# Attention blocks 2 to 7: layernorm statistics by ScalarE in two accumulating passes, x transposed by 32x32 squares and DMA moves, denominators inverted in a narrow layout

## The chip, the cores and the metric

The kernel runs on one core of a Trainium2 chip. The engines of a core work side by side: TensorE (PE) multiplies matrices into PSUM, VectorE (DVE) and ScalarE (ACT) work on elements, GpSimd (POOL) does a few small operations and issues some of the DMA transfers, SyncE (SP) issues most of them. The metric is the device time of one execution in microseconds (us); less is better.

## The reference

x holds 8 batches of 512 tokens with 512 features in float32. Four parts follow one another, each added to x behind a learned gate:

```python
x = x + tanh(g_xattn[0]) * xattn0(layernorm(x), ctx)      # linear attention, 16 heads of 32
x = x + tanh(g_ffn[0])   * ffn0(layernorm(x))             # 512 -> 2048 -> 512, exact gelu
x = x + tanh(g_xattn[1]) * xattn1(layernorm(x), ctx, mask)# softmax over 64 memory tokens
x = x + tanh(g_ffn[1])   * ffn1(layernorm(x))             # 8 expert groups, top 8 of 32, silu
```

The change touches the first of them alone. There, with f(y) = y + 1 where y > 0 and exp(y) elsewhere:

```python
q    = f(x_norm @ Wq.T)                      # per head
gate = sigmoid(x_norm @ Wg.T + bg)
k, v = f(ctx @ Wk.T), ctx @ Wv.T
z    = 1 / (q . sum_of_k + 1e-6)             # one number per token and head
out  = (q @ (k.T @ v)) * z * gate @ Wo.T
```

## The kernel before, in words

The work is cut into three times eight blocks, one per batch: `xa0` (the linear attention), then `ff0`, then `ff1` (which begins with the softmax attention). A block's x stands in SBUF as 128 partitions x 4 token tiles x 512 features. The large products are computed on PE by a scheme of seven half-size products in place of eight (numbered 1 to 7 in the code; their sums and differences are formed by DVE and ACT). Each `xa0` block has three of them: `QUp` (tiles x_q, w_q, z_q), `GUp` (x_g, w_g, z_g) and `ODown` (x_xa_down, w_xa_down, z_xa_down). Products 1, 6 and 7 of Q and G are copied out of PSUM by ACT (line 928, tiles u1, u6, u7); every product of O is added into x by DVE (line 1048).

The main loop (lines 1409 to 1468) runs over b. Turn b issues Q of block b, G of block b, and O of block b - 1, since O needs the denominators z of its block. Between the products it calls generators: `prep` (`prep_xa0` of block b + 1, which is `normed` and then `token_combinations`), `den` (`denominators`), `gated`, `numerators`, `attended`, and a `builder` that forms weight sums for the ff0 stage on DVE, with loads and stores on SP.

`normed` (lines 475 to 586) makes the normalised and transposed x of a block, xnT. In `xa0` blocks it takes mean and variance of each token by DVE (bn_stats and bn_aggr, four tiles), lets POOL raise the variance to the power -1/2, and normalises on ACT (line 60 in the profile, bias and scale per token). Each normalised tile is transposed by four PE transposes into PSUM (line 524, pt_xa), and ACT copies the result to xnT (line 526). The second way in the same function, used by most blocks of the later stages, has ACT write the tile in a layout of 32x32 squares, DVE transpose the squares in place (line 562), and 16 DMAs of 64 KB move the rows to their partitions. `token_combinations` (lines 680 to 696) forms four sums S of the quarters of xnT on DVE.

`denominators` (lines 1247 to 1266) multiplies q by the sums of the keys on PE (pd, 128 x 512, each of 16 heads repeated in eight rows), adds the small constant and inverts on DVE (lines 1255 and 1258), and stores the 128 x 512 result to DRAM by SP. `spread` reads it back with each head's row copied to the 32 partitions of its features.

The order of instructions on an engine is set before the run. A scheduler with its own cost model orders PE, DVE and ACT in this phase; instructions issued inside `with here("vector")` or the like, and all of POOL's and SP's, keep the order of the program among themselves. Every instruction of an engine waits for those before it. Line 60 is the helper through which such ordered instructions are recorded, so that many groups of the profile carry that line.

Of the kernel before, what the change touches and what calls it, by code (L numbers as in the profile page):

```python
# [30 lines left out]
P = 128  # L31
# [37 lines left out]
def flamingo_kernel(  # L69
# [46 lines left out]
    bank = {"ps": ps, "xn": awork}  # L116
# [110 lines left out]
    for h in range(P // HD):  # L227
        nc.vector.memset(heads[ts(h, HD), ts(h, 8)], 1.0)
    neg_half = const.tile([P, NT], F32, tag="neg_half", name="neg_half")
# [245 lines left out]
    def normed(ph, b, tag, normed_part=lambda t: None):  # L475

        xb = xs[ph, b]
        by_products = ph == "xa0" or tag == "ff0_0"
        xnT = work.tile([P, NC, S] if ph == "xa0" else [P, NC, NT, P], F32, tag="xnT", name=f"xnT_{tag}")
# [3 lines left out]
        ahead = held or ph == "xa0" and b > 0  # L483
        with here(*(["vector"] if held or ph == "xa0" else [])):
            for t in range(NT):
                st = small.tile([P, 6], F32, tag="st", name=f"st_{tag}_{t}")
                nc.vector.bn_stats(st, xb[:, t, :])  # L487
                nc.vector.bn_aggr(mv[:, t, :], st)
        var = small.tile([P, NT], F32, tag="var", name=f"var_{tag}")
        nc.vector.tensor_scalar(var, mv[:, :, 1], LN_EPS, None, ALU.add)  # L490
        rstd = small.tile([P, NT], F32, tag="rstd", name=f"rstd_{tag}")
        if by_scalar:
            shift = small.tile([P, NT], F32, tag="nshift", name=f"nshift_{tag}")
            nc.vector.tensor_scalar(shift, mv[:, :, 0], -1.0, None, ALU.mult)  # L494
# [20 lines left out]
        if by_products:  # L515

            def normed_tile(t):
                xn[t] = bank["xn"].tile([P, D], F32, tag="xn", name=f"xn_{tag}_{t}", bufs=2)
                norm(t, xn[t])

            def turn(t):
# [3 lines left out]
                if ph == "xa0":  # L525
                    nc.scalar.copy(xnT[:, :, ts(t, P)], pt)
# [31 lines left out]
        xn = bank["xn"].tile([P, NC, NT, P], F32, tag="xn", name=f"xn_{tag}")  # L558
# [1101 lines left out]
```

## Time and profile before

| | |
|---|---|
| time, three runs | 2025.08, 2026.78, 2028.16 us; median 2026.78 |
| the profiled execution | 2028.04 us, of which the span of instructions is 2026.3 |
| granted PE clock, mean | 0.999 |
| busy, whole span | PE 99%, PE's weight loads 88%, DVE 75%, ACT 32%, POOL 11% |
| the attention stretch | about 50 to 372 us of the span |

A row of the groups by line reads: line, engine, operation, what is written from what, partitions x elements, how many; then busy us and mean ns of one; then the engine's idle time just ahead of them and what ended it. In a row of the waits, the engine and tile on the left stood idle for what is on the right: us in total, number of times, the longest. A row of the timeline has start, duration, engine, line and instruction; ends of matmuls are modelled, so that the distance from one start to the next says more than the durations.

### The profile page before, as it was taken

How to read it: one execution, taken by the hardware profiler on the slowest of the kernel's cores; microseconds unless marked ns; L12 is line 12 of the kernel's file. 1: busy time of each engine (PE TensorE's matmuls, PEld its weight loads, DVE VectorE, ACT ScalarE, POOL GpSimd, SP SyncE). 2: the span in 40 equal slices, each digit the busy share in tenths (PEclk: the TensorE clock that was granted, in tenths of full speed). 3: DMA queues.
4: the chain of work that ended last, by engine and by line, in shares of the span. 5: the costliest groups of instructions: out<-in, count | busy, mean ns of one | idle time of the engine just before them, and what ended most of it. 6: DMA issues, size and time to landing. Idle time of an engine off the chain costs nothing. (4 is left out here: it accounts for less than half of the span.)

```text
span 2026.3 us, 35088 instructions
## 1 busy us (share of the span) xinstructions
PE 2004.3 (99%) x12428; PEld 1779.3 (88%) x12428; DVE 1509.6 (75%) x3012; ACT 648.2 (32%) x1294; POOL 216.8 (11%) x387
## 2 busy tenths in 40 slices
PE   9999999999999999999999999999999999999998
PEld 5888887899989899999888889898989888898988
DVE  4688888676857677777767687787788786877758
ACT  3543443323242424233234231313232232313121
POOL 3000000101010101011011111110202020110000
PEclk9999999999999999999999999999999999999999
DMA  6466655799999999999987969696978879696865
GB/s 202 138 206 189 186 161 166 235 319 292 317 291 300 301 302 279 299 301 287 296 266 247 307 206 304 204 307 194 305 236 250 277 227 304 191 318 181 280 202 171
DMA packets 318062, 508.81 MB, mean 251 GB/s; under 512 B 42945, under 2 KB 109665, under 8 KB 313793
## 3 DMA queue, kind: packets, MB, share of 16 engines
q1 hardware_dynamic: 302768, 464.05, 72.9%
q0 software_dynamic: 9264, 19.31, 3.5%
q10 hardware_dynamic: 5856, 23.20, 3.2%
q8 instruction: 101, 1.65, 0.3%
q14 instruction: 73, 0.59, 0.1%
HBM read 413.04 MB, written 69.27 MB: 238 GB/s over the span
## 5 line engine op out<-in xcount | busy, mean ns | idle before, releaser
L916 PE MATMUL x_ff<-S_ff,w_ff 128*128 128x256 f32 x1280 | 303.0, 380 | 2.4 <-ACT u_ff L928 2.4
L916 PE MATMUL w_ff<-S_ff,w_ff 128*128 128x256 f32 x1280 | 303.9, 380 | 0.5 <-DVE a_ff L971 0.3
L916 PE MATMUL x_ff<-xnT_ff,w_ff 128*128 128x256 f32 x1280 | 298.5, 381 | 0.0
L928 ACT COPY u_ff<-x_ff 128x512 f32<-128x512 f32 x240 | 140.0, 584 | 447.8 <-PE x_ff L916 412.7
L916 PEld LDWEIGHTS x_ff<-S_ff,w_ff 128*128 128x128 f32 x1280 | 242.7, 190 | 35.5 <-ACT u_ff L928 2.8
L916 PEld LDWEIGHTS w_ff<-S_ff,w_ff 128*128 128x128 f32 x1280 | 241.0, 190 | 36.7 <-issue 2.7
L916 PEld LDWEIGHTS x_ff<-xnT_ff,w_ff 128*128 128x128 f32 x1280 | 240.4, 191 | 33.9 <-issue 2.1
L1111 PE MATMUL x_ff_down<-w_ff_down,split_ff_down 128*128 128x128 f32 x1344 | 162.5, 275 | 1.1 <-DVE split_ff_down L1096 0.9
L1111 PEld LDWEIGHTS x_ff_down<-w_ff_down,split_ff_down 128*128 128x128 f32 x1344 | 156.0, 192 | 1.6 <-DVE split_ff_down L1096 1.1
L916 PE MATMUL z_ff<-xnT_ff,w_ff 128*128 128x256 f32 x640 | 153.1, 380 | 0.0
L1125 DVE TENSOR_TENSOR part_ff_down<-part_ff_down 128x128 f32<-128x128 f32 x315 | 85.1, 289 | 71.3 <-ACT part_ff_down L1138 62.0
L916 PEld LDWEIGHTS z_ff<-xnT_ff,w_ff 128*128 128x128 f32 x640 | 119.8, 190 | 20.6 <-issue 5.3
L495 POOL TENSOR_TENSOR rstd_ff<-var_ff,neg_half 128x4 f32<-128x4 f32 x15 | 15.9, 1061 | 861.7 <-DVE nshift_ff L494 861.7
L1111 PE MATMUL w_ff_down<-w_ff_down,split_ff_down 128*128 128x128 f32 x896 | 107.9, 275 | 0.0
L1111 PEld LDWEIGHTS w_ff_down<-w_ff_down,split_ff_down 128*128 128x128 f32 x896 | 103.9, 192 | 0.0
L976 ACT ACTIVATE a_ff<-a_ff,b_sb 128x256 f32<-128x256 f32 x128 | 58.1, 501 | 92.5 <-DVE a_ff L971 92.5
L1009 DVE TENSOR_TENSOR up_ff<-w_ff,u_ff 128x512 f32<-128x512 f32 x96 | 65.8, 685 | 27.1 <-ACT u_ff L928 27.1
L971 DVE TENSOR_TENSOR a_ff<-w_ff,u_ff 128x512 f32<-128x512 f32 x64 | 44.0, 687 | 54.9 <-ACT u_ff L928 54.4
L1111 PE MATMUL x_ff_down<-w_ff_down,a_ff 128*128 128x128 f32 x672 | 83.5, 275 | 1.0 <-ACT a_ff L60 1.0
L1111 PE MATMUL w_ff_down<-w_ff_down,s_ff 128*128 128x128 f32 x672 | 82.8, 275 | 0.0
L1111 PEld LDWEIGHTS x_ff_down<-w_ff_down,a_ff 128*128 128x128 f32 x672 | 79.7, 192 | 1.8 <-ACT a_ff L60 1.1
L999 DVE SCALAR_TENSOR_TENSOR g_ff<-th_ff,x_ff 128x512 f32<-128x512 f32 x48 | 32.7, 681 | 64.8 <-ACT th_ff L998 64.8
(264 smaller groups left out, 3462.0 us busy)
## 6 DMA issues: line engine op xcount, KB each, us to landing
w_ff_down<-stream_ff SPq DMA_DIRECT2D x680, 256.0 KB
w_ff<-ff_up SPq DMA_DIRECT2D x560, 256.0 KB
stream_ff<-build_ff_down SPq DMA_DIRECT2D x49, 448.0 KB
x_ff<-x_ff SPq DMA_DIRECT2D x16, 1024.0 KB
share<-shares SPq DMA_DIRECT2D x64, 256.0 KB
ff_up<-build_ff_up SPq DMA_DIRECT2D x42, 256.0 KB
x_ff<-x_xa ACTq DMA_DIRECT2D x8, 1024.0 KB
x_ff<-x_ff ACTq DMA_DIRECT2D x8, 1024.0 KB
```

The costliest lines, as they stand in the source:

```text
L495: nc.gpsimd.tensor_tensor(rstd, var, neg_half, ALU.pow)
L916: nc.tensor.matmul(p[:, n, :], lhsT=w[:, c, ts(n, P)], rhs=moving, **self.mark(m, 2 * n + c),)
L928: nc.scalar.copy(self.s[m], p)
L971: nc.vector.tensor_tensor(h, p, s, ALU.add)
L976: nc.scalar.activation(h[:, n, :], p[:, n, :], AF.Gelu, bias=b1_sb[:, f : f + 1])
L999: nc.vector.scalar_tensor_tensor(g, th, 1.0, p, ALU.add, ALU.mult)
L1009: nc.vector.tensor_tensor(u, p, s, ALU.add)
L1111: nc.tensor.matmul(p[bank][:, place, :], lhsT=operand[k][:, c, :], rhs=w[at // 4][:, ts(at % 4, P)], start=bank not in opened, stop=True, ...
L1125: return lambda: nc.vector.tensor_tensor(m(k), m(k), m(by), ALU.add)
```

## The change

Four things change, all in `xa0`.

1. In blocks 2 to 7 the statistics come from ACT. A first pass (Identity with an accumulator, four tiles) gives the sums, DVE turns them into the shift, a second pass (Square with the shift as bias, four tiles) gives the sums of squares; DVE makes the variance of them. Power, shift and normalisation follow as before.
2. In the same blocks x is transposed in the second way of `normed`: squares on DVE, and 16 DMAs, here issued by SP. All `xa0` blocks take over the layout of xnT that the later stages have. Blocks 0 and 1 keep bn_stats and the PE transposes.
3. For blocks 0 to 6 the denominators go from PSUM through ACT (constant added), one row per head by a POOL DMA to DRAM, back as 128 x 64 by a second POOL DMA, through one DVE reciprocal of 128 x 64, and out by a third POOL DMA. `spread` reads 16 rows in place of 128. Block 7 keeps the wide reciprocal and stores 16 rows.
4. The main loop calls `prep` after other products: after Q's n = 0, 1, 3, 4 (at b = 0 only 4) in place of 4, after G's 0, 1, 2 in place of 3, and after O's 1 in place of 0, 1, 3, 5, with the remainder at O's 4.

```diff
--- before.py
+++ after.py
...
     def normed(ph, b, tag, normed_part=lambda t: None):
 
         xb = xs[ph, b]
-        by_products = ph == "xa0" or tag == "ff0_0"
-        xnT = work.tile([P, NC, S] if ph == "xa0" else [P, NC, NT, P], F32, tag="xnT", name=f"xnT_{tag}")
+        by_products = tag in ("xa0_0", "xa0_1", "ff0_0")
+        xnT = work.tile([P, NC, NT, P], F32, tag="xnT", name=f"xnT_{tag}")
         mv = small.tile([P, NT, 2], F32, tag="mv", name=f"mv_{tag}")
         held = ph == "ff0" and b > 1
         by_scalar = tag != "xa0_0"
         ahead = held or ph == "xa0" and b > 0
+        var = small.tile([P, NT], F32, tag="var", name=f"var_{tag}")
+        rstd = small.tile([P, NT], F32, tag="rstd", name=f"rstd_{tag}")
+        if ph == "xa0" and not by_products:
+            sums = small.tile([P, 2, NT], F32, tag="sums", name=f"sums_{tag}")
+            shift = small.tile([P, NT], F32, tag="nshift", name=f"nshift_{tag}")
+            with here():
+                for t in range(NT):
+                    nc.scalar.activation(
+                        temp(f"of_{tag}_{t}"), xb[:, t, :], AF.Identity, accum_out=sums[:, 0, t : t + 1]
+                    )
+            yield
+            nc.vector.tensor_scalar(shift, sums[:, 0], -1.0 / D, None, ALU.mult)
+            with here():
+                for t in range(NT):
+                    nc.scalar.activation(
+                        temp(f"off_{tag}_{t}"),
+                        xb[:, t, :],
+                        AF.Square,
+                        bias=shift[:, t : t + 1],
+                        accum_out=sums[:, 1, t : t + 1],
+                    )
+            yield
+            nc.vector.tensor_scalar(var, sums[:, 1], 1.0 / D, LN_EPS, ALU.mult, ALU.add)
         with here(*(["vector"] if held or ph == "xa0" else [])):
-            for t in range(NT):
+            for t in range(NT if by_products or ph != "xa0" else 0):
                 st = small.tile([P, 6], F32, tag="st", name=f"st_{tag}_{t}")
                 nc.vector.bn_stats(st, xb[:, t, :])
                 nc.vector.bn_aggr(mv[:, t, :], st)
-        var = small.tile([P, NT], F32, tag="var", name=f"var_{tag}")
-        nc.vector.tensor_scalar(var, mv[:, :, 1], LN_EPS, None, ALU.add)
-        rstd = small.tile([P, NT], F32, tag="rstd", name=f"rstd_{tag}")
-        if by_scalar:
-            shift = small.tile([P, NT], F32, tag="nshift", name=f"nshift_{tag}")
-            nc.vector.tensor_scalar(shift, mv[:, :, 0], -1.0, None, ALU.mult)
+        if by_products or ph != "xa0":
+            nc.vector.tensor_scalar(var, mv[:, :, 1], LN_EPS, None, ALU.add)
+            if by_scalar:
+                shift = small.tile([P, NT], F32, tag="nshift", name=f"nshift_{tag}")
+                nc.vector.tensor_scalar(shift, mv[:, :, 0], -1.0, None, ALU.mult)
         nc.gpsimd.tensor_tensor(rstd, var, neg_half, ALU.pow)
         if by_scalar:
             nc.gpsimd.tensor_tensor(shift, shift, rstd, ALU.mult)
...
-                xn[t] = bank["xn"].tile([P, D], F32, tag="xn", name=f"xn_{tag}_{t}", bufs=2)
+                if tag == "xa0_0":
+                    xn[t] = start.tile([P, D], F32, tag="xn", name=f"xn_{tag}_{t}", bufs=2)
+                elif tag == "xa0_1":
+                    if t == 0:
+                        xn["all"] = aunits.tile([P, NT, D], F32, tag="a", name=f"xn_{tag}")
+                    xn[t] = xn["all"][:, t, :]
+                else:
+                    xn[t] = temp(f"xn_{tag}_{t}")
                 norm(t, xn[t])
 
             def turn(t):
                 pt = psum(f"pt_{tag}_{t}").rearrange("p (c q) -> p c q", q=P)
                 for c in range(NC):
                     nc.tensor.transpose(pt[:, c, :], xn[t][:, ts(c, P)], ident)
-                if ph == "xa0":
-                    nc.scalar.copy(xnT[:, :, ts(t, P)], pt)
-                else:
-                    nc.scalar.copy(
-                        xnT[:, :, t].rearrange("p q (c i) -> p c q i", c=NC),
-                        pt.rearrange("p c (q i) -> p c q i", q=NC),
-                    )
+                nc.scalar.copy(
+                    xnT[:, :, t].rearrange("p q (c i) -> p c q i", c=NC),
+                    pt.rearrange("p c (q i) -> p c q i", q=NC),
+                )
 
...
-        xn = bank["xn"].tile([P, NC, NT, P], F32, tag="xn", name=f"xn_{tag}")
+        xn = bank["xn"].tile([P, NC, NT, P], F32, tag=bank["tag"], name=f"xn_{tag}")
...
                 with here("gpsimd"):
-                    queue = nc.sync if tag.startswith("ff1") else nc.gpsimd
+                    queue = nc.sync if ph == "xa0" or tag.startswith("ff1") else nc.gpsimd
                     queue.dma_start(out=xnT[ts(l, HD), q], in_=xn[ts(q, HD), l])
...
-    def features_of(ph, xnT):
-
-        if ph == "xa0":
-            return xnT.rearrange("p c (t q i) -> p c t q i", q=NC, i=HD)
+    def features_of(xnT):
+
         return xnT.rearrange("p q t (c i) -> p c t q i", c=NC)
...
-        if ph == "xa0":
-            v = features_of(ph, xnT).rearrange("p c t q i -> p c t (q i)")
-            a11, a12, a21, a22 = (v[:, ts(h, 2), ts(r, 2)] for r in range(2) for h in range(2))
-            to = s.rearrange("p k c (t i) -> p k c t i", t=2)
-        else:
-            a11, a12, a21, a22 = (xnT[:, :, ts(r, 2), ts(h, 2 * HD)] for r in range(2) for h in range(2))
-            to = s.rearrange("p k c (q t i) -> p k (c q) t i", q=2, t=2)
+        a11, a12, a21, a22 = (xnT[:, :, ts(r, 2), ts(h, 2 * HD)] for r in range(2) for h in range(2))
+        to = s.rearrange("p k c (q t i) -> p k (c q) t i", q=2, t=2)
         nc.vector.tensor_tensor(to[:, 0], a21, a22, ALU.add)
         nc.vector.tensor_tensor(to[:, 1], to[:, 0], a11, ALU.subtract)
         nc.vector.tensor_tensor(to[:, 2], a11, a21, ALU.subtract)
         nc.vector.tensor_tensor(to[:, 3], a12, to[:, 1], ALU.subtract)
-        if ph == "xa0":
-            return to.rearrange("p k c t (q i) -> p k c t q i", i=HD)
         return to.rearrange("p k q t (c i) -> p k c t q i", c=2)
...
         z = temp(f"z_{b}")
-        nc.vector.tensor_scalar(z, pd, ATT_EPS, None, ALU.add)
-        yield
-        for r in range(2):
-            nc.vector.reciprocal(z[:, ts(r, H2)], z[:, ts(r, H2)])
+        of_heads = z.rearrange("(n k) t -> n k t", k=8)[:, 0, :]
+        over[b] = dram.tile([P // 8, S], F32, tag=f"over{b}", name=f"over_{b}")
+        if b == B - 1:
+            nc.vector.tensor_scalar(z, pd, ATT_EPS, None, ALU.add)
             yield
-        over[b] = dram.tile([P, S], F32, tag=f"over{b}", name=f"over_{b}")
-        nc.sync.dma_start(out=over[b], in_=z)
+            for r in range(2):
+                nc.vector.reciprocal(z[:, ts(r, H2)], z[:, ts(r, H2)])
+                yield
+            nc.sync.dma_start(out=over[b], in_=of_heads)
+            yield
+            return
+        nc.scalar.activation(z, pd, AF.Identity, bias=eps, scale=1.0)
+        under = dram.tile([P // 8, S], F32, tag=f"under{b}", name=f"under_{b}")
+        narrow = small.tile([P, S // 8], F32, tag="narrow", name=f"narrow_{b}")
+        with here("gpsimd"):
+            nc.gpsimd.dma_start(out=under, in_=of_heads)
+            nc.gpsimd.dma_start(out=narrow, in_=under.rearrange("n (u q) -> (n u) q", u=8))
+        yield
+        yield
+        nc.vector.reciprocal(narrow, narrow)
+        with here("gpsimd"):
+            nc.gpsimd.dma_start(out=over[b].rearrange("n (u q) -> (n u) q", u=8), in_=narrow)
+        yield
         yield
 
     def spread(b):
 
-        rows = over[b].rearrange("(c h k) t -> c k h t", c=NC, k=8)
+        rows = over[b].rearrange("(c h) t -> c h t", c=NC)
         over[b] = aunits.tile([P, NC, S], F32, tag="over", name=f"spread_{b}")
         for h in [slice(0, 2), slice(2, 4)] if b == B - 1 else [slice(0, 4)]:
             for c in range(NC):
-                nc.sync.dma_start(out=over[b][ts(c, HD), h], in_=rows[c, 0, h].partition_broadcast(HD))
+                nc.sync.dma_start(out=over[b][ts(c, HD), h], in_=rows[c, h].partition_broadcast(HD))
...
+    bank.update(xn=aunits, tag="over")
...
             if n == 4:
                 flush()
-                if b < B - 1:
-                    some(prep)
+            if n in ((4,) if b == 0 else (0, 1, 3, 4) if b < B - 1 else ()):
+                some(prep)
             tick()
         if done:
             attended(done[0], done[2], numerators(*done[0:2]))
...
                     load_x("ff0", 1)
             if b == B - 1 and n > 3:
                 next(den, None)
-            if n == 3 or n > 3 and not done:
+            if n in ((0, 1, 2) if b < B - 1 else (3,)) or n > 2 and not done:
                 some(prep)
         if not done:
             for _ in den:
...
             elif n == 6:
                 attended(b, g.th, pn, gated)
                 combine_inner(slice(0, 2), "x")
-            if n in ((0, 1, 3, 5) if b < B - 1 else (6,)):
+            if n in ((1,) if b < B - 1 else (6,)):
                 some(prep)
+            if n == 4 and b < B - 1:
+                for _ in prep:
+                    pass
             tick()
         for _ in prep:
             pass
...
```

More of the change, by code (lines that the diff above doesn't have):

```diff
@@ L115, in flamingo_kernel @@
     kvp = first.enter_context(tc.tile_pool(name="kvp", bufs=2, space=PSUM))
-    bank = {"ps": ps, "xn": awork}
+    bank = {"ps": ps}
     def psum(name):
@@ L228, in flamingo_kernel @@
         nc.vector.memset(heads[ts(h, HD), ts(h, 8)], 1.0)
+    eps = const.tile([P, 1], F32, tag="eps", name="eps")
+    nc.vector.memset(eps, ATT_EPS)
     neg_half = const.tile([P, NT], F32, tag="neg_half", name="neg_half")
@@ L737, in cross_attention @@
                     lhsT=ctxT[:, c, :],
-                    rhs=features_of("ff1", xnT)[:, c].rearrange("p (u r) q i -> p r u q i", r=2)[:, r],
+                    rhs=features_of(xnT)[:, c].rearrange("p (u r) q i -> p r u q i", r=2)[:, r],
                     start=c == 0,
@@ L797, in prep_ff1 @@
                     lhsT=router_sb[:, c, :],
-                    rhs=features_of("ff1", xnT)[:, c, t],
+                    rhs=features_of(xnT)[:, c, t],
                     start=c == 0,
@@ L902, in product @@
             xnT, s = blocks[self.ph, self.b][0:2]
-            v = features_of(self.ph, xnT)
+            v = features_of(xnT)
             (w,) = self.weights(m)
@@ L1535, in flamingo_kernel @@
     hpool = stack(tc.tile_pool(name="inner", bufs=1, reuse_waits="tile"))
-    bank["xn"] = hpool
+    bank.update(xn=hpool, tag="xn")
     router_sb = hpool.tile([P, NC, E], F32, tag="router_w", name="router_sb")
```

## The prediction

> **What bounds the kernel now.** I read the page's head, then the waits of TensorE (PE) from 0 to 400 us, the stretch that holds the attention blocks, then the groups by line there, then timelines.
>
> ```profile
> span 2026.3 us, 35088 instructions
> ...
> PE 2004.3 (99%) x12428; PEld 1779.3 (88%) x12428; DVE 1509.6 (75%) x3012; ACT 648.2 (32%) x1294; POOL 216.8 (11%) x387
> ```
>
> PE works 99% of the span; 22 us in all are idle. Time is won only by taking instructions off PE or ending one of its few waits, and any new wait of PE lengthens the span one for one. Its waits in this stretch, and the groups that the change touches:
>
> ```profile
> PE x_g L916 <- ACT u_g L928: 1.8, 3, 1.2
> ...
> PE pd L60 <- DVE q L673: 1.1, 1, 1.1
> PE x_xa_down L1032 <- DVE x_xa L1048: 0.8, 1, 0.8
> ```
>
> ```profile
> L1258 DVE RECIPROCAL z<-z 128x256 f32<-128x256 f32 x16 | 27.4, 1734 | 0.2
> ...
> L60 DVE BATCH_NORM_STATS2 st_xa<-x_xa 128x6 f32<-128x512 f32 x32 | 21.4, 667 | 0.7 <-DMA x_xa<-in_x 0.7
> ...
> L524 PE MATMUL pt_xa<-ident,xn_xa 128*128 128x128 f32 x112 | 17.3, 277 | 0.1
> ...
> L526 ACT COPY xnT_xa<-pt_xa 128x512 f32<-128x512 f32 x28 | 16.2, 579 | 20.3 <-PE pt_xa L524 20.3
> ```
>
> Only pt_xa is PE's. PE's timeline at a block's end (start, duration) gives its price, and shows what stands between two O products:
>
> ```profile
> 230.70 1.89 PE L1032 MATMUL w_xa_down<-w_o,s_xa 128*128 128x256 f32 x8
> 232.43 0.60 PE L524 MATMUL pt_xa<-ident,xn_xa 128*128 128x128 f32 x4
> 232.87 1.89 PE L1032 MATMUL x_xa_down<-w_o,a 128*128 128x256 f32 x8
> 234.59 1.89 PE L916 MATMUL x_q<-xnT_xa,w_q 128*128 128x256 f32 x8
> 236.32 1.89 PE L1032 MATMUL x_xa_down<-w_o,a 128*128 128x256 f32 x8
> ```
>
> A product takes 1.73 us from start to start, four transposes 0.43 to 0.49.
>
> **The change part by part.** What stands where comes from the order in which the changed program's instructions stand on each engine.
>
> *Transposes off PE.* Blocks 2 to 7 lose 16 transposes each, four times 0.44 = 1.76 us a block: 6 x 1.76 = 10.6 us gained (14.8 at most, were all 96 on the path at 17.3/112 = 0.154). The ACT copies (28 x 0.58) and the DVE statistics end beside PE's work and give nothing directly.
>
> *Waits that end.* The normalising ACT instructions stood just ahead of u_g copies and waited for a POOL power that took up to 4.19 us. In the changed order they stand otherwise, so some of the 1.8 us on u_g goes; between 0 and 1.8 I take 1.2.
>
> *ScalarE's two passes.* The eight passes stand on ACT after the u1_q copy and ahead of the u6_q copy, which Q's seventh product needs in order to start. Widths of 512 cost 0.63 (fe_q, no bias) and 0.80 (bias and scale, xn_xa); Square with a bias lies between, 0.71. The accumulator adds a read (in the only accumulating group, sc on L759: 32 activations of 341 ns on average, 32 reads of 188), but those pairs started 0.33 us apart, so I take it as overlapped. From the start of x_q's first product: u1 starts at 1.93 (194.16 to 196.09 in the timeline), first pass 2.42 to 4.94, the shift on DVE to 5.25 (0.17 and two hand-overs), second pass to 8.1, u6 to 8.7. PE wants it at 6.9 plus whatever O work stands after that first product. That is 1.30, 0.86, 1.73, 1.30 and 3.46 us in blocks 2 to 6, so waits of 0.5, 0.9, 0.1, 0.5 and 0: 2.0 us. If the reads don't overlap, eight of them add 1.5 a block, up to 8 us; if ACT is a little quicker it is 0.
>
> *O's products back to back.* Before, x_q stood between the last two x_xa_down products (232.87 and 236.32). In loops 1 to 4 of the changed order they follow one another, and the second accumulates over a bank that DVE (L1048) must first empty. Before has this once, at the end:
>
> ```profile
> 372.43 1.99 PE L1032 MATMUL x_xa_down<-w_o,a 128*128 128x256 f32 x8
> 375.27 0.92 PE L1032 MATMUL x_xa_down<-w_o,a 128*128 128x256 f32 x3 [0.84 <-DVE x_xa L1048]
> ```
>
> 375.27 - 372.43 - 1.73 = 1.1 us: four times, 4.4. In block 7 the pt_ff between two such products moves too: 0.9 more (0 to 1). Sum 5.3, bounds 3.4 (the idle 0.84 alone) and 5.4.
>
> *Narrow reciprocals.* Two of 1734 ns on DVE become one of 64 columns, some 0.45 us, but it waits on two POOL DMAs in series (z to DRAM, DRAM to 128x64) while standing in DVE's fixed order ahead of the eviction of O's sixth product, which the seventh needs. With the end of pd as zero, ACT has z at 0.97, and PE wants that seventh product at 8.65; behind the reciprocal stand 0.45 and the 0.75 eviction and hand-overs. So the wait is what the two landings exceed 6.35 us by. The nearest rows are POOL's small transfers in the later stages:
>
> ```profile
> L60 POOL DMA_DIRECT2D ctxd<-in_ctx x16: 516/526/603, 964.8 to 1763.5; - x16
> ...
> DMA to landing us min/median/max: 2.8/3.8/7.2
> ```
>
> and ctxdT 3.3, 4.1 and 7.7. Both minima give 6.1 and no wait, both medians 7.9 and 1.55 us. The new transfers are a quarter the size of ctxd; I take 7.0, so 0.65 us in each of blocks 1 to 6: 3.9. Both maxima would give 8.5 a block, 51. The DMA that stores the result, and the spread behind it on SP, have some 3 us to spare before the gating of Q's early products.
>
> *The first block.* narrow_0's reciprocal stands ahead of S and of block 2's shift on DVE. From the end of block 1's first Q product it can run at about 7.4, the shift ends at 8.3, the second pass at 11.2, two tanh of 0.5 at 12.0, u6 at 12.6, wanted at 8.65: 4.0 us once; between 1 (both landings short, S alone) and 6 (landings at 9).
>
> *Moves on SP.* Sixteen DMAs of 64 KB follow the DVE transposes, and the loads and stores for the weight sums queue behind them on SP. Issues took 0.59 us each at the median (16 in ff1 in 11.2 us). DVE's transposes (0.70 each) end 9 to 10 us after G's first product starts, so they land at 22 to 24 us, and Q wants them at 25 to 27: hidden by G and O, with 1 to 3 us to spare. Nothing for it, up to 2 us a block if not. The strided reads of xnT cost nothing: ff's products on that layout run at the same 380 ns.
>
> *Split pd.* pd no longer runs together with other small groups; four more changes between tile shapes at 0.15 (the product at 341.31, after pd, took 0.1 longer, and pd itself costs some on entry): 0.6.
>
> Sum: -10.6 - 1.2 + 2.0 + 5.3 + 3.9 + 4.0 + 0.6 = +4.0 us. The profiled execution took 2028.04 (span 2026.3 and 1.7 around it), 1.3 over the median 2026.78. 2032.0 by it, 2031 against the median.
>
> **Two rules weighed.** POOL's own work depends on what DVE is doing, by this row: the same power took 1.006 us in one block and 4.19 in another.
>
> ```profile
> L60 POOL TENSOR_TENSOR rstd_xa<-var_xa,neg_half x8: 1006/1211/4192, 22.4 to 293.8; 128x4 f32<-128x4 f32 x8
> ```
>
> The Trainium skill (SBUF — State Buffer, "A bandwidth-pool intuition that's wrong") says that a transfer issued by GpSimd waits for its descriptors while DVE holds the shared port, 3.1 us in place of 0.62: 2.5 more for each of two transfers would add 5 us to six blocks, +30, and end at 2061. The same skill's DMA: Bandwidth & Descriptors ("Anatomy of one DMA — SWDGE (gpsimd) path") gives a fixed 2.0 us for such a transfer: 4.1 for the two, no wait at the reciprocal, and 2027. No row here shows a lone 32 KB transfer between busy DVE instructions, so my sum stays with the landings above.
>
> **The rivals.**
> - *The gain comes through (faster).* The landings stay under 6.35, the reciprocal of the first block costs 1, ACT's passes 1: -11.8 + 1 + 4.4 + 0 + 1 + 0.6 = -4.8: 2022. For it: the minima 2.8 and 3.3, and that DVE loses about 3 us a block, which gives room. Against: the back-to-back O products, in the order whatever the DMAs do. It decides at landings of 6.35.
> - *POOL's transfers are slow (slower).* At 5.6 each (the smallest at the start, gates_in, took 5.6 and 5.9 with others ahead) the two take 11.2, 4.85 us a block, 29 in place of 3.9: 2056; in half of the blocks, 2043. For it: maxima of 7.2 and 7.7. Against: those were queued, these are alone.
> - *The moved x lands late on SP (slower).* 16 issues of up to 0.7 us and DVE's transposes 2 us late eat the 3 us, and PE stands at x_q. S then holds up evictions behind it on DVE too. 2 us in six blocks: 2043. For it: issues in ff1 took up to 1.4. Against: SP was busy for 29 of the 48 us from 192 to 240.
>
> **How the numbers follow.** 0.2% (4 us) is about what can be told from no change here. The forecast has 0.42: 2031, own range 2024 to 2039; its centre lies on the bound of 0.2%, so of it 0.24 is slower, 0.15 the same, 0.03 faster. The gain coming through has 0.32 (0.28 faster, 0.04 the same), slow transfers 0.14 and late x 0.12, both slower. Faster 0.31, same 0.19, slower 0.50. The range goes down to 2017 (the transposes at 10.6, u_g's 1.8, O's 3.4 and little else: 2018) and up to 2046, past 2043, and leaves out the upper end of slow transfers.
>
> **What would show it.** In the changed profile pt_xa x16 and PE some 10 us less busy; waits of PE at x_q on u_q (2 us, and 4 more in one block), x_xa_down on DVE x_xa four or five times near 0.9, and again longer where the reciprocal is late; the landings of under and narrow add to 7. No wait on xnT or on spread. I am wrong if the two landings are far from 7, if xnT is late, or if the accumulating passes cost other than 0.63 and 0.71.

## The result, and the profile after

The changed kernel takes 2032.33 us (median of 9 runs, 2030.25 to 2035.21) against 2025.08 for the kernel before (median of 9 runs, 2023.34 to 2028.16): a ratio of 1.0034, 95% interval 1.0025 to 1.0043, so 5 to 9 us slower. The profiled execution took 2031.77 us with a span of 2030.0. That of before, with 2028.04, lay 3 us over its own median, so that the two spans, 3.7 us apart, show less than the whole difference. The stages show it better.

The page's head of the changed kernel:

```profile
span 2030.0 us, 35185 instructions
...
PE 1999.1 (98%) x12332; PEld 1767.7 (87%) x12332; DVE 1483.8 (73%) x2975; ACT 670.8 (33%) x1373; POOL 225.2 (11%) x408
```

PE lost 96 instructions and 5 us of busy time, and the span grew: its idle time rose from 22 to 31 us. The waits of PE from 0 to 410 us, same columns as before:

```profile
PE x_xa_down L1051 <- DVE x_xa L1067: 6.5, 8, 0.9
PE x_q L935 <- ACT u_q L947: 3.5, 4, 2.0
PE x_g L935 <- ACT u_g L947: 2.1, 1, 2.1
...
PE pt_xa L555 <- ACT xn_xa L60: 1.5, 2, 0.9
```

The reader is to see that the first two rows, small before (0.8 and, for u_q, nothing), are now the largest. The one row with a DMA, which is left out here, is 1.6 on w_k, a load of weights at the start that took 1.1 before: what was moved to queues is not waited for. The groups that answer to those of before:

```profile
L500 ACT ACTIVATE off_xa<-x_xa,nshift_xa 128x512 f32<-128x512 f32 x24 | 17.0, 710 | 3.5 <-DVE nshift_xa L497 3.5
L60 DVE STREAM_TRANSPOSE xn_xa<-xn_xa 128x512 f32<-128x512 f32 x24 | 15.9, 688 | 0.0
...
L493 ACT ACTIVATE of_xa<-x_xa 128x512 f32<-128x512 f32 x24 | 14.8, 620 | 0.0
...
L1293 DVE RECIPROCAL narrow<-narrow 128x64 f32<-128x64 f32 x7 | 3.8, 545 | 0.4 <-DMA narrow<-under 0.4
```

To place the loss I cut PE's timeline at the first G product of each block. It stands at the same place of every turn, behind five of the block's seven Q products. "First" runs from z_g of block 0 to x_g of block 1, the turns 1 to 6 from one x_g to the next, "last" from x_g of block 7 to the first product of ff0. The sum is called the mark from here on; it leaves out the time up to z_g, which differed by up to 3 us between kernels that begin alike (57.5 to 60.6).

| us | first | 1 | 2 | 3 | 4 | 5 | 6 | last | mark |
|---|---|---|---|---|---|---|---|---|---|
| before | 24.0 | 40.4 | 41.9 | 41.3 | 40.4 | 40.4 | 41.1 | 49.5 | 319.0 |
| after | 28.9 | 41.1 | 42.1 | 41.2 | 41.6 | 39.9 | 41.1 | 50.5 | 326.3 |

The mark moved by 7.3 us, the whole of the difference of the medians. A turn without waits takes 40.43 with the PE transposes and, less four times 0.43, 38.7 without them. So turns 1 to 6 gave up 14.7 us over that floor. Where, PE's timeline says. In turn 4:

```profile
236.76 1.89 PE L1051 MATMUL x_xa_down<-w_o,a 128*128 128x256 f32 x8
239.50 1.99 PE L1051 MATMUL x_xa_down<-w_o,a 128*128 128x256 f32 x8 [0.84 <-DVE x_xa L1067]
241.33 0.59 PE L1051 MATMUL w_xa_down<-w_o,s_xa 128*128 128x256 f32 x2
241.76 1.89 PE L935 MATMUL x_q<-xnT_xa,w_q 128*128 128x256 f32 x8
```

Two x products of O stand together, 2.74 apart in place of 1.73: 1.0 to 1.1 in each of turns 1 to 4, 4.1 in all, and 0.4 more by the slower products behind them (1.83 from start to start here). In the same kernel and view, pd in turn 5:

```profile
263.95 1.89 PE L1051 MATMUL x_xa_down<-w_o,a 128*128 128x256 f32 x8
265.77 1.04 PE L1270 MATMUL pd<-q,ksum 128*32 128x512 f32 x2
266.74 1.99 PE L935 MATMUL x_g<-S_xa,w_g 128*128 128x256 f32 x8
268.67 1.06 PE L60 MATMUL pd<-q,ksum 128*32 128x512 f32 x6
269.65 1.13 PE L1051 MATMUL z_xa_down<-w_o,a 128*128 128x256 f32 x4
```

pd's eight matmuls took 0.99 in one piece. Here two of them take 0.97, the product between gets 0.2 longer, and the other six take 0.98: 1.2 us more, without any wait that a list would show. This is in turns 2 to 5; in turn 1 pd's pieces follow one another but take 1.57, 0.6 more. That makes 5.3. The waits on u_q come to 2.3 in turns 1, 2 and 4 with the slower product that follows each, the one on u_g in turn 6 to 2.4. Together 14.5 of the 14.7. The first turn adds 4.9 (its wait on u_q 2.3, those on pt_xa 1.5, and pd, which is cut there too, 1.2), the last 1.0; the floor's gain of 10.3 and the 3.0 of waits that before had in turns 2, 3 and 6 stand against it.

### The profile page after: what moved, and what is told of

The parts are those of the page before. It is cut to its first block, busy times and chain, and to the rows that moved or that the text cites. A ratio compares the mean times of both kernels' runs of the same rounds, so it can differ in the third digit from the quotient of the medians.

```text
span 2030.0 us, 35185 instructions
## 1 busy us (share of the span) xinstructions
PE 1999.1 (98%) x12332; PEld 1767.7 (87%) x12332; DVE 1483.8 (73%) x2975; ACT 670.8 (33%) x1373; POOL 225.2 (11%) x408
## 4 chain that ended last, share of the span: by engine, by line
PE 92%; DVE 3%; ACT 2%; DMA 2%; issue 1%; POOL 0%; SPq 0%; DVEq 0%; ACTq 0%; POOLq 0%
PE x_ff L935 27%; PE w_ff L935 13%; PE x_ff_down L1130 13%; PE w_ff_down L1130 9%; PE z_ff L935 7%; PE z_ff_down L1130 4%; PE v_ff_down L1130 4%; PE x_xa_down L1051 2%; PE x_q L935 2%; PE x_g L935 2%; PE w_g L935 1%; PE w_xa_down L1051 1%; PE pst L754 1%; PE pr L799 1%; PE pv L60 1%
## 5 line engine op out<-in xcount | busy, mean ns | idle before, releaser
L1130 PEld LDWEIGHTS w_ff_down<-w_ff_down,s_ff 128*128 128x128 f32 x672 | 80.0, 192 | 0.8
```

Of the source, the lines that this page charges most:

```text
L1130: nc.tensor.matmul(p[bank][:, place, :], lhsT=operand[k][:, c, :], rhs=w[at // 4][:, ts(at % 4, P)], start=bank not in opened, stop=True, ...
```

## The experiments

The question was whether these are separate losses with separate causes, and which of the change's parts bring them. Besides the ratio to before, each run is read by its turns:

| us | first | 1 | 2 | 3 | 4 | 5 | 6 | last | mark | ratio to before |
|---|---|---|---|---|---|---|---|---|---|---|
| e1_wide | 28.4 | 39.9 | 41.2 | 41.4 | 43.7 | 43.8 | 40.2 | 52.1 | 330.7 | 1.0055 (1.0038 to 1.0073) |
| e2_pd | 27.9 | 41.0 | 45.5 | 40.5 | 40.5 | 38.9 | 41.1 | 50.4 | 325.7 | 1.0024 (1.0014 to 1.0033) |
| e3_first | 24.8 | 42.1 | 41.2 | 41.6 | 41.6 | 39.9 | 42.8 | 50.5 | 324.5 | 1.0023 (1.0013 to 1.0033) |
| e4_oorder | 30.2 | 41.1 | 41.5 | 41.0 | 40.9 | 39.9 | 41.1 | 50.7 | 326.3 | 1.0036 (1.0023 to 1.0048) |
| e5_own7 | 30.5 | 41.1 | 42.1 | 41.2 | 41.6 | 39.9 | 44.9 | 50.5 | 331.7 | 1.0064 (1.0047 to 1.0081) |
| e6_dvestats | 27.2 | 41.2 | 41.5 | 41.0 | 41.4 | 40.4 | 39.9 | 50.5 | 323.1 | 1.0023 (1.0013 to 1.0032) |
| e7_pet | 30.4 | 40.5 | 40.4 | 40.4 | 40.4 | 40.4 | 40.4 | 49.3 | 322.3 | 1.0005 (0.9995 to 1.0014) |
| e8_four | 24.0 | 41.8 | 43.4 | 41.4 | 41.0 | 40.4 | 43.4 | 50.7 | 326.1 | 1.0040 (1.0026 to 1.0055) |
| e9_pet_first | 24.8 | 40.4 | 40.4 | 40.4 | 40.4 | 40.4 | 40.4 | 49.3 | 316.6 | 0.9993 (0.9984 to 1.0002) |
| e10_dve_fixed | 23.9 | 38.7 | 40.2 | 39.4 | 42.2 | 40.8 | 40.3 | 52.3 | 318.0 | 0.9994 (0.9985 to 1.0003) |
| e11_narrow | 23.9 | 40.4 | 42.3 | 40.4 | 40.4 | 40.4 | 40.8 | 53.9 | 322.7 | 1.0016 (1.0006 to 1.0025) |
| e12_stats | 24.3 | 40.6 | 40.7 | 40.4 | 40.4 | 40.4 | 40.5 | 49.1 | 316.4 | 0.9991 (0.9982 to 1.0000) |

Each row is one profile. In some of them a wait of PE was followed by a stretch at a lower clock (last section), and 1.3 to 3 us of the turn belong to that: turn 5 of e1_wide, turn 2 of e2_pd, turn 6 of e3_first and e5_own7, the first turns of e4_oorder, e5_own7 and e7_pet, and the last of e11_narrow.

In the expectations of e1 to e4 the mark is still the start of ff0 in the trace's own time (378.8 before, 384.9 in the changed kernel); from e5 on it is counted from z_g, as here. Each expectation numbers its own theories.

### e1_wide: the wide inversion back

```diff
-        if b == B - 1:
+        if True:
             nc.vector.tensor_scalar(z, pd, ATT_EPS, None, ALU.add)
```

> The changed kernel with the denominators inverted as before (DVE adds the constant and inverts 128 x 512 in two halves, SP stores 16 rows) in all blocks. The mark for all these runs is the start of ff0's first product: 378.8 in the kernel before, 384.9 in the changed one. Theory 1 (the narrow inversion costs PE nothing by itself, its two landings being 2.0 and 2.1 us; what it does is to change the order that the scheduler writes: in this kernel's order x_q stands again between O's last two x products in every block): the four waits of 1.0 us there go, the rest stays, 381 to 382, ratio about 1.001 to 1.002. Theory 2 (the reciprocal behind two transfers held up DVE's queue, as the prediction had it at 3.9 us, and 2 of the first block's 4): those go too, 376 to 378. Theory 3 (the 3 us a block that DVE got back were needed, now that it turns squares): 386 or later.

Theory 3 fits: ff0 begins at 388.5. Theory 1's effect is there too (turn 1 loses its waits and 1.2 us), but in turns 4 and 5 PE waits on DVE's evictions of O longer than ever. PE's timeline of this run, two of its lines:

```profile
236.12 1.99 PE L1051 MATMUL x_xa_down<-w_o,a 128*128 128x256 f32 x8 [1.83 <-DVE x_xa L1067]
...
279.34 2.79 PE L1051 MATMUL x_xa_down<-w_o,a 128*128 128x256 f32 x8 [1.95 <-DVE x_xa L1067]
```

DVE was busy for 189.7 us of the stretch from 90 to 330 (173.1 in the changed kernel). So with squares on DVE the narrow inversion helps: by 4.4 us of the mark here, some 1.7 of them the lower clock in turn 5. That its own reciprocal delays PE nowhere in the changed kernel is told by its row above: it waited 0.4 us for a landing, once, and no wait of PE follows from it. The cost of 3.9 that the prediction put on it was not there.

### e2_pd: pd kept together

```diff
-        for c in range(NC):
+        for c in (2, 3, 0, 1):
             nc.tensor.matmul(pd[ts(c, HD), :], lhsT=kv[b][1][:, c, :], rhs=q[:, c, :], start=True, stop=True)
```

> The changed kernel with pd's four products over q's feature groups written in the order 2, 3, 0, 1, so that the first of them already needs the part of q that comes last, and the four stay together (in the order they do so in all blocks but the first). Theory 1 (in the profile after, pd is split around a product of G in turns 2 to 5, where its pieces can't share the array, and each split costs 0.5 to 1.3 us, 4.3 in all): the mark moves from 384.9 to about 381, and one of the four waits between O's products goes as well by the order, 380. Theory 2 (the split only filled time in which PE would have waited for the last part of q): pd waits in one piece instead, within 1 us of 384.9.

In turns 3, 4 and 5, 0.7, 1.2 and 1.0 us went with the split; turn 5 came to 38.9, the floor. Theory 1 holds for these. Turn 2 lost 3.5 to a wait that was not there before, on a qs_q by which DVE takes a product of Q out of PSUM:

```profile
141.80 2.01 PE L1051 MATMUL x_xa_down<-w_o,a 128*128 128x256 f32 x6 [4.38 <-DVE qs_q L1236]
```

(PE's timeline.) From 134.7 to 141.1 DVE had multiplications of a, transposes and weight sums in its queue ahead of that qs. So the order that kept pd together moved PE's wait, and the whole gained 0.6.

### e3_first: the first turn's steps as before

```diff
-            if n in ((0, 1, 2) if b < B - 1 else (3,)) or n > 2 and not done:
+            if n in ((0, 1, 2) if 0 < b < B - 1 else (3,)) or n > (2 if b else 3) and not done:
                 some(prep)
```

> The changed kernel with the steps of preparation in the first turn (b = 0) placed after G's products as before the change (from the fourth on), the other turns as they are. Theory 1 (the first turn lost 4.9 us from z_g of block 0 to x_g of block 1, 24.0 before and 28.9 after: block 1's PE transposes were moved ahead of where their input is ready, 1.5 us of waits with their refills, and block 2's passes on ACT now stand ahead of the u6_q copy, 2.0): the two waits go, the first turn takes 24 to 25, the mark comes to 381. Theory 2 (it is the passes on ACT and the layout copy alone, wherever they stand): the first turn stays at 27 to 29.

The first turn took 24.75, 4.2 less: Theory 1. Its wait on pt_xa is gone and the one on u_q is 0.3. The later turns lost 2.3 of it: with other steps the scheduler wrote another order for turn 1, and turn 6 took 1.7 longer (told below, among the things not expected).

### e4_oorder: O's products in another order

```diff
-            parts = {1: (1, 1), 2: (1, 1), 6: (1, 2), 7: (2, 2), 4: (2, 1), 3: (1, 2)}
-            todo = [(parts[m], p)] if m in parts else []
-            if m == 7:
-                todo.append(((2, 2), self.banks["w"]))
+            parts = {1: (1, 1), 2: (1, 1), 6: (1, 2), 5: (2, 2), 7: (2, 2), 4: (2, 1), 3: (1, 2)}
+            todo = [(parts[m], p)]
...
     class ODown(Down):
+        order = (1, 2, 6, 5, 7, 3, 4)
```

> The changed kernel with O's seven products in the order 1, 2, 6, 5, 7, 3, 4 and the w bank emptied right after product 5, so that product 3 stands between the two x products whose bank DVE has to empty in between; the arithmetic is the same. Theory 1 (the wait of 0.84 to 0.94 and its refill is paid in turns 1 to 4, 1.0 to 1.1 each, and twice at the end): no such wait in turns 1 to 4, the mark at 380 to 381. Theory 2 (DVE is late there for other reasons, the reciprocal and S ahead of it in its queue, and PE waits for the same eviction one product later): the waits stay under another name, 384 to 385.

The waits between O's products are gone in turns 1 to 4, and the turns gained only 0.1, 0.6, 0.2 and 0.7. PE's waits of this run, 0 to 400 us:

```profile
PE x_q L935 <- ACT u_q L947: 4.8, 4, 2.0
PE x_g L935 <- ACT u_g L947: 2.1, 1, 2.1
PE x_xa_down L1051 <- DVE x_xa L1065: 1.9, 2, 1.1
```

The row of u_q rose from 3.5 to 4.8: while PE stood at O, ACT was working off its passes, and without that wait PE comes to u6 earlier by as much. Neither theory had this: the second named DVE, and it was ACT.

### e5_own7: another tile for block 7

```diff
+        if tag == "xa0_7":
+            xn = work.tile([P, NC, NT, P], F32, tag="x", name=f"xn_{tag}", bufs=3)
+        else:
+            xn = bank["xn"].tile([P, NC, NT, P], F32, tag=bank["tag"], name=f"xn_{tag}")
-        xn = bank["xn"].tile([P, NC, NT, P], F32, tag=bank["tag"], name=f"xn_{tag}")
```

> The changed kernel, with block 7's normalised x in a free slot of the tiles for x in place of the tile that it shares with the spread denominators. The mark is from here on the time from z_g of block 0 to the first product of ff0, which leaves out differences of the start: 319.0 us before, 326.3 changed. Theory 1 (in turn 6 ACT's four normalising instructions wait 2.3 us for the gating on DVE, L1310, that still reads the shared tile, then hold up u_g's copy for 2.1 us): the wait on u_g goes, turn 6 takes 38.8 in place of 41.1, the mark is 324. Theory 2 (it is the place of the four instructions on ACT, ahead of that copy, whatever they waited for): the wait on u_g stays, over 1.5 us.

Turn 6 took 44.9, not 38.8, with some 1.6 of it a lower clock behind the second of these waits. PE's timeline:

```profile
300.16 1.99 PE L938 MATMUL x_q<-xnT_xa,w_q 128*128 128x256 f32 x8 [1.14 <-ACT u_q L950]
...
311.87 3.58 PE L938 MATMUL x_g<-S_xa,w_g 128*128 128x256 f32 x8 [2.81 <-ACT u_g L950]
```

ACT's timeline of this run:

```profile
298.12 1.52 ACT L60 ACTIVATE xn_xa<-x_xa,nshift_xa,rstd_xa 128x512 f32<-128x512 f32 x2 [3.68 <-DMA x_ff<-x_xa]
299.55 0.56 ACT L950 COPY u_q<-x_q 128x512 f32<-128x512 f32 x1
...
310.71 0.63 ACT L700 ACTIVATE fe_q<-qs_q 128x512 f32<-128x512 f32 x1 [4.85 <-DVE qs_q L1239]
311.25 0.57 ACT L950 COPY u_g<-x_g 128x512 f32<-128x512 f32 x1
```

So the run does not decide between the theories. The new tile brought a wait of its own, 3.7 us for a store (x_ff) ahead of the first normalising instruction, and a u_q copy stands behind that. The copy of u_g stands behind an fe_q for which ACT sat idle, waiting for DVE. In the changed kernel that is the same:

```profile
304.93 0.63 ACT L697 ACTIVATE fe_q<-qs_q 128x512 f32<-128x512 f32 x1 [1.96 <-DVE qs_q L1236]
305.47 0.57 ACT L947 COPY u_g<-x_g 128x512 f32<-128x512 f32 x1
```

There the four normalising instructions take 2.9 us in a row and end at 301.2, well before. DVE works without a gap from 295.1 on, and block 7's four squares are among what stands ahead of that qs_q. So the wait on u_g in turn 6 is DVE's lateness, handed on by ACT; what of it the tile or the normalising brought stays open.

### e6_dvestats: statistics on DVE

The function normed loses the two passes; bn_stats and bn_aggr run for all blocks:

```diff
-            for t in range(NT if by_products or ph != "xa0" else 0):
+            for t in range(NT):
                 st = small.tile([P, 6], F32, tag="st", name=f"st_{tag}_{t}")
```

> The changed kernel with the statistics of blocks 2 to 7 by DVE's bn_stats again; squares, moves and narrow inversion stay. Theory 1 (the eight passes on ACT ahead of the u6_q copy cost 0.4 to 0.9 us in turns 1, 2 and 4 and 2.0 and more in the first): no wait on u_q, the mark is 322 to 323. Theory 2 (DVE, which has the squares now, can't take 3.4 us more a block, as run e1_wide showed for the 3.0 us of the reciprocals: there waits of 1.8 to 2.0 us on DVE came up in turns 4 and 5): 328 to 333.

Theory 1: the row of u_q falls from 3.5 to 0.3 and the mark by 3.2. DVE bears it, at 187.0 us busy of the 240 from 90 to 330, with single waits up to 1.2. O's waits are still there, and so is pd cut in two.

### e7_pet: PE transposes back

```diff
-        by_products = tag in ("xa0_0", "xa0_1", "ff0_0")
+        by_products = ph == "xa0" or tag == "ff0_0"
+        by_dve = tag in ("xa0_0", "xa0_1")
...
-            if n in ((0, 1, 2) if b < B - 1 else (3,)) or n > 2 and not done:
+            if n in ((0, 1, 2) if b == 0 else () if b < B - 1 else (3,)) or n > 2 and not done:
...
-            if n in ((1,) if b < B - 1 else (6,)):
+            if n in ((0, 1, 3, 5) if b < B - 1 else (6,)):
```

(by_dve stands where by_products chose the kind of statistics; the rest of the transposes ends at O's n = 6.)

> The changed kernel with all of xa0 transposed by PE again, in the steps of the loop where the kernel before has them; statistics by ACT and the narrow inversion stay, so does the new layout of xnT. PE's order is then that of the kernel before but for the first turn. Theory 1 (the moves' own consequences, O's products back to back, split pd, the shared tile, take more than the 10.6 us that the transposes give): the first turn stays at 28 to 29, turns 1 to 6 take 40.4 each without the waits on u_q, and the mark is 322 to 324, below the changed kernel's 326.3. Theory 2 (the losses belong to the statistics and the inversion, and the transposes' gain is real and kept): 10 us more than the changed kernel, 336.

Theory 1, and plainly: with 10 us more of work on PE the mark is 4.0 lower than the changed kernel's, and turns 2 to 6 take 40.43 each. PE's waits of this run, from the top:

```profile
PE x_xa_down L1052 <- DVE x_xa L1068: 3.2, 3, 1.5
PE x_q L936 <- ACT u_q L948: 2.0, 1, 2.0
PE pt_xa L556 <- ACT xn_xa L60: 1.5, 2, 0.9
```

All of the second and third row is in the first turn, the first row in the last. Statistics and narrow inversion leave no wait in turns 1 to 6, as long as PE's order is the old one. The run puts back the transposes and the places of `prep` in the loop together; squares at the old places were not run, so which of the two brings PE's worse order is not shown.

### e8_four: four waits ended at once

The edits of e3_first, e4_oorder and e5_own7, and the second pass behind the u6_q copy:

```diff
-            if n in ((4,) if b == 0 else (0, 1, 3, 4) if b < B - 1 else ()):
+            if n in ((4,) if b == 0 else (0, 2, 3, 4) if b < B - 1 else ()):
                 some(prep)
```

> The changed kernel with four edits: the first turn's steps as in e3_first, O's order as in e4_oorder, block 7's own tile as in e5_own7, and the second pass of the statistics issued after Q's third product (n = 2) in place of the second, behind the u6_q copy. Theory 1 (the losses are separate waits): first turn 24.5, no waits between O's products, none on u_q of more than 0.3, none in turn 6; what is left is pd's splits, 39.3 a turn: the mark at 24.5 + 6 x 39.3 + 50.5 = 311, ratio to before 0.996. Theory 2 (each wait that goes is taken up by the next, as in e4_oorder, where four waits of 1.0 went and the turns gained 1.9 in all): 317 to 321, ratio 0.999 to 1.001.

Worse than either theory. The first turn came to 24.0, but PE waits 1.7 on u_q in turn 1, 2.4 on a copy of Q by ACT in turn 2, 1.2 on u_q in turn 3, and 1.3 on u_q and 2.8 on u_g in turn 6. The last edit did not reach its aim: in ACT's timeline of this run the second pass still stands ahead of the u6_q copy in every turn (in turn 1 it ends at 120.15, and the copy starts there). And the wait on u_g has ACT idle ahead of it, for 4.9 us, on a qs_q by DVE, as in e5_own7.

### e9_pet_first: PE transposes, and the first turn as before

In e7_pet, the first turn's steps of prep as before the change:

```diff
-            if n in ((0, 1, 2) if b == 0 else () if b < B - 1 else (3,)) or n > 2 and not done:
+            if n in (() if 0 < b < B - 1 else (3,)) or n > 3 and not done:
```

> e7_pet (PE transposes everywhere, statistics by ACT, narrow inversion) with the first turn's steps placed as before the change. Theory 1 (e7_pet's only loss was the first turn, 30.4 us against 24.0, while its turns 1 to 6 took 40.43 each and were 3 us shorter in all than before): the first turn takes 24 to 25, the mark is 316 to 317 against 319.0 before, ratio to before 0.997 to 0.999. Theory 2 (the passes on ACT hold up the first turn wherever they stand): first turn 27 or more, ratio 1.000 or more.

Theory 1 in the profile: first turn 24.75, no wait of 0.4 us or more up to the last turn, mark 316.6. In the time it is 0.9993 of before, with an interval that still holds 1.

### e10_dve_fixed: squares with the other waits ended

The edits of e6_dvestats, e2_pd, e4_oorder and e3_first together.

> The changed kernel with four edits: statistics by bn_stats on DVE as in e6_dvestats, pd's products in the order of e2_pd, O's order of e4_oorder, the first turn's steps of e3_first; squares, moves and narrow inversion stay. Theory 1 (with the ACT passes gone, each of the other waits can be ended by itself): first turn 24 to 25, turns 1 to 6 at 38.7 to 39.5, the mark 308 to 312, ratio 0.994 to 0.997. Theory 2 (DVE and ACT are so close behind PE in these turns that a wait that is ended comes back elsewhere, as in e4_oorder and e8_four): turns of 40 to 41.5, the mark 317 to 322, ratio 0.999 to 1.002.

Theory 2 by its mark, 318.0, and its ratio; the turns spread wider than it said, from 38.7 to 42.2. Turn 1 shows that the floor can be reached (38.7), and turn 4 (42.2) that it isn't kept: in turns 3 to 6 stand waits on DVE of 0.5 to 1.8 us (q for pd, O's evictions, qs) and one of 0.9 on ACT. Eight us better than the changed kernel, and no better than leaving the squares out.

### e11_narrow and e12_stats: one part alone

e11_narrow is the kernel before with the changed denominators and spread (the tile narrow is a slice of a temporary one, for space). e12_stats is e9_pet_first with the wide inversion, by the edit of e1_wide.

> The kernel before with the third part of the change alone: the denominators of blocks 0 to 6 by ACT, POOL's DMAs and one narrow reciprocal (its tile taken from the temporary ones, for space); everything else as before, PE's order too. Theory 1 (its two landings of 2.0 and 2.1 us leave 2 us to spare, and it takes 3 us a turn off DVE): turns of 40.4 to 41.9 as before or shorter, the mark 316 to 319, ratio 0.998 to 1.000. Theory 2 (the prediction's third step: the reciprocal waits in DVE's queue in front of O's eviction, 0.65 us a block): the mark 322 to 323, ratio 1.001 to 1.002.

> The statistics of blocks 2 to 7 by ACT alone of the change's parts (with the new layout of xnT): PE transposes, wide inversion on DVE, the first turn's steps as before. It differs from e9_pet_first by the inversion only, and from the kernel before by the statistics. Theory 1 (the passes fit on ACT where Q's first product is followed by two products of O, and taking 3.4 us a turn off DVE is what ended the waits of turns 2, 3 and 6 in e9_pet_first): turns of 40.4 throughout, first turn 24 to 25, the mark at 316 to 318, as e9_pet_first. Theory 2 (the narrow inversion, with its 3 us off DVE, did that): waits of 0.5 to 1.5 in turns 2, 3 and 6 as before the change, the mark at 319 to 320.

e11_narrow came to Theory 2's mark, and not by its way: four of the six turns take 40.43, as Theory 1 has it. The reciprocal waited for its landing in six of seven blocks, 12.1 us in all, and in turn 2 alone that reached PE, as the prediction's term for the narrow reciprocal has it. DVE's timeline of this run:

```profile
147.33 0.55 DVE L1276 RECIPROCAL narrow<-narrow 128x64 f32<-128x64 f32 x1 [4.47 <-DMA narrow<-under]
```

and PE's:

```profile
149.79 1.99 PE L1034 MATMUL x_xa_down<-w_o,a 128*128 128x256 f32 x8 [1.61 <-DVE x_xa L1050]
```

The two landings took some 4.3 us each there (their maxima in this run are 4.2 and 4.4). DVE was busy for only 1.4 of the 10 us from 138 to 148, so it was not DVE that held them up. The last turn is 4.5 us longer than before: O's evictions stand behind S of ff0 in DVE's order, PE waits 3.3, and the two products behind that wait run at a clock of 0.50, which is 3.0 us. Without that stretch the mark would stand at 319.7, next to Theory 1's. Why the order came out so is not shown.

e12_stats: Theory 1. Turns at the floor with transposes, mark 316.4, ratio 0.9991 with 1.0000 as the upper end of its interval. PE's waits, 0 to 400 us, from the top:

```profile
PE idle L60 <- DVE heads L60: 1.1, 1, 1.1
PE pd L60 <- DVE q L700: 1.1, 1, 1.1
PE x_xa_down L1052 <- DVE x_xa L1068: 0.8, 1, 0.8
```

No u_q, no u_g: the statistics on ACT are enough to end the waits of before in turns 2, 3 and 6 (where they cost 3.0). They are not needed for it: e11_narrow, without them, has no wait on u_g either. It was the squares, with the places of `prep` that came with them, that took this and more.

## Why the prediction was right, and where not

It forecast 2031, slower than before; 2032.33 came. The sum, +4.0, is too small by 3.3 us against the 7.3 that were measured; the forecast came nearer than that only because its base, 2026.78, was 1.7 above the median of 2025.08. The terms fared differently.

- **Transposes, 10.6 gained: right.** The floor of a turn fell by 1.71 (38.72 in turn 1 of e10_dve_fixed against 40.43), 10.3 for six.
- **Waits on u_g, 1.2 gained: half right.** Before's are gone, and were worth 2.6 with the slower products behind them. A new one of 2.1 (2.4 with its product) stands in turn 6, where DVE, at block 7's squares, is late with a qs_q and ACT has u_g's copy behind it (e5_own7). That was not seen.
- **ACT's passes, 2.0: right.** The waits were 0.36, 0.79, 0, 0.36 and 0 in blocks 2 to 6 (from start to start 0.52, 0.95, 0.09, 0.52 and 0.09 lost) where the working had 0.5, 0.9, 0.1, 0.5 and 0. The passes took 620 and 710 ns, and the reads lay under the next pass.
- **O's products together, 4.4 and 0.9: right**, 4.1 and, for block 7's pair, 1.1.
- **The narrow reciprocal, 3.9: wrong, nothing.** This is the step that failed: it took the landings at 7.0 us. The mechanism exists (e11_narrow), its size came from the wrong rows. The landings of the tile under and of the tile narrow in the changed kernel:

```profile
DMA to landing us min/median/max: 1.8/2.0/3.0
```

```profile
DMA to landing us min/median/max: 1.7/2.1/3.6
```

4.1 together by the medians, where 6.35 was free and 7.0 assumed; the prediction had named landings far from 7 as a sign of being wrong. ctxd's 3.8 is the landing of transfers four times as large that stand in other traffic. Of the two rules weighed, the Trainium skill's DMA: Bandwidth & Descriptors ("Anatomy of one DMA — SWDGE (gpsimd) path"), about 2.0 us for a small transfer, agrees with 2.0 and 2.1 here. The lock of SBUF — State Buffer ("A bandwidth-pool intuition that's wrong"), by the prediction's estimate from that page 2.5 us more, isn't seen: with DVE busy for 173 of 240 us the longest of fourteen landings is 3.6.
- **The first block, 4.0: near in sum (4.9), wrong in make.** The u6 wait was 2.0, since the reciprocal ran at once; 1.5 of waits on block 1's own transposes, moved ahead with the same line of the loop, and 1.2 for pd cut in two were left out. That the sums agree is luck.
- **x by SP, nothing: right.** The profile has no landing times for these transfers; that they cost nothing is told by PE's waits, where no row names xnT.
- **pd's split, 0.6: the term that was mis-sized most: 5.3** in turns 1 to 5, and 1.2 in the first. A pd that is cut costs 1.2, not 0.15: its two parts take 0.97 and 0.98, each as long as the whole did.

So 3.9 too much at the reciprocal and 1.4 too little gained at u_g stand against 4.7 too little at pd, 2.4 in turn 6 and 0.9 in the first turn. With the reciprocal at nothing and the rest as it was, the sum would have been +0.1, no change: that the forecast said slower rests on the term that was wrong, and what made the kernel slower in its place were pd and turn 6. The direction was luck in part, and so was the closeness. Of the rivals, the first ("the gain comes through") had the landings right and failed at pd, at turn 6 and in the first turn, which it had at 1; slow transfers and late x didn't come.

## What to carry to other kernels

Work taken off the engine that is the bound pays only if what replaces it leaves that engine's order intact: here 10.3 us of transposes went, and the new order of PE and new waits on ACT and DVE took 14.7 in the same turns. Between engines that are near their limit a wait that is ended can come back at the next one (e2_pd, e4_oorder); read the turn, not the wait. And ask of a wait on one engine what that engine itself waited for (e5_own7). Small matmuls that run side by side in a group are to be counted as a group: cut in two it cost twice here, and no list of waits tells it.

## What was not expected of the hardware

After a wait of PE of about 2 us or more, the product behind it sometimes runs at about half speed. In e3_first, PE's timeline in turn 6:

```profile
302.27 3.56 PE L935 MATMUL x_g<-S_xa,w_g 128*128 128x256 f32 x8 [2.10 <-ACT u_g L947]
```

against the changed kernel at the same place, after the same wait:

```profile
306.08 1.99 PE L935 MATMUL x_g<-S_xa,w_g 128*128 128x256 f32 x8 [2.09 <-ACT u_g L947]
```

The table by windows of e3_first (columns: window, length, busy time of PE, its loads, DVE, ACT and POOL, granted PE clock, DMA share, GB/s) has the clock that was granted:

```profile
302.20:304.00 1.80, 1.73 (x5) 1.40 (x6) 1.77 (x4) 1.34 (x4) 0.00 (x0) 0.59 0.46 112
304.00:306.00 2.00, 2.00 (x7) 1.60 (x5) 0.80 (x2) 0.14 (x1) 0.00 (x0) 0.51 0.30 73
306.00:308.00 2.00, 2.00 (x12) 1.30 (x14) 0.98 (x2) 1.24 (x3) 0.00 (x0) 1.00 0.40 98
```

So a wait of 2.1 us cost 3.9 in one execution and 2.4 in another, with the product behind it. The same is seen in e5_own7 after 2.02 (0.58) and 2.81 us (0.59), in e7_pet and e4_oorder after 2.02 (0.50), in e11_narrow after 3.33 (0.50), in e2_pd after 4.38 (0.64) and, the shortest, in e1_wide after 1.95 (0.50; its row at 279.34 is above). In e8_four waits of 2.41 and 2.81 had a product of 1.99 behind them. The Trainium skill's TensorE: Matmul & The Clock Gate ("What's actually happening") describes a clock halved after an idle window of 3.4 us that runs freely. That the drop comes in some executions and not in others fits this; that 1.95 us were enough does not, and the measurement decides. The turns of the table that carry such drops are named below it.
